# The last image's last stages, row block by row block beside the last scan

## The chip, the cores and the metric

The kernel runs on one core of one Trainium2 chip. The metric is the device time of one launch in microseconds (us); the figure given for a kernel is the median of several runs. The profile is one execution recorded by the hardware profiler, and its times count from the start of its span.

Engines are named as in the profile: PE (TensorE, with PEld for its weight loads), DVE (VectorE), ACT (ScalarE), POOL (GpSimd) and SP (SyncE). SP issues nearly all DMAs of this kernel, in program order.

## The reference

Four images of 96 channels and 64 x 64 points pass through four residual layers. Layer 0 is an attention block, layer 1 and layer 3 each contain a state-space scan in four directions, layer 2 is a 3 x 3 convolution. What matters here is the end of layer 3, after its scan. `oy` holds the four directions; 0 and 2 run along rows (forward and backward), 1 and 3 along columns:

```
y = oy[:, 0] + inv[:, 0] + why + invwhy               # sum over the four directions, 192 channels
y = layernorm_last(y) ; x1 = (y * silu(z)) @ ow.T     # to 96 channels
y = x1 + x2 * g ; y = layernorm over the channels
# crm: squeeze to 24 + 24 channels, a grouped 3x3 convolution, two 1x1 ones,
#      softmax over the channel means of the whole image, a weighted sum
out = y @ fin_w.T + fin_b ; x = x + out
```

Everything up to the convolution works on points; the convolution needs the neighbouring image rows; the softmax needs the means over the whole image, and the output comes after it. The order in which the four directions are added does not matter for what is computed.

## The kernel before, in words

An image is a tile of 96 partitions by 4096 points; 192 channels are two halves `h`. Small stages work on eight chunks of 512 points, that is eight image rows each (`PCH`).

**The scans.** There are eight scans (`SCANS`: layer 1 and layer 3 of each image), each made of 32 groups: four directions, four chunks of 1024 points, two halves. A group has 12 steps, so a scan has 384 steps and the program 3072. A step is `unit(i)`: it asks for the decay tile `rep` of step i+4 (`fetch`, L1807), makes the decays of step i+2 on ACT (`decays`, L1815), runs the scan itself on DVE (`scan`, L1836), multiplies by the output coefficients on POOL (`times_c`, L1848), lets PE sum three steps (`collect`) and spread the inputs of step i+2 into the PSUM tile `bx` (`drive`), and multiplies on DVE (`times_b`, L1829). After a group, `output` forms `yo` and the store to `y_row` or `y_col` in DRAM goes out one step later (L1884). Backward directions first read back what the forward one stored (L1858) and add to it. The order of directions is written out in `KINDS`; for both layers rows come first, columns last.

**The work beside.** The other stages of the images are generators: `first` (layer 0), `second` (end of layer 1, layer 2, start of layer 3) and `third` (end of layer 3). `BESIDE` names which of them run beside which scan. Their code is cut by `yield` into slots. `Slots.begin(budget)` runs one slot ahead of the step's other instructions or in its middle, `end` runs its second half; each slot has a cost, and each step receives `PACE` = 3.5 of budget (less 2.1 in every third step). The generator `prepare`, which makes the inputs of the group after next, is served by the same slots. All instructions of an engine stand in the order in which this program emits them (`manual_schedule`). At step `per - NG - LEAD - 1` = 365 of a scan, `work.run()` emits whatever is left of the work beside it, since the next scan needs its results.

**The end of layer 3.** `third(b)` is `directions` followed by `finish`. `directions` loads the column sums of a half image into `yc` and the row sums into `V`, and POOL adds the turned `yc` to `V` (L1371). `finish` normalizes (`layer_norm`, with `gate` after each chunk), projects, normalizes again (with `squeeze` after each chunk), convolves, sums for the softmax, scales the last weights and writes the output (`o`, L1667, stored in L1669). Each stage goes through all eight chunks before the next begins. The loads of a chunk (`xz`, `x2`, `o`) are issued in the slot that uses them.

The last scan is that of layer 3 of image 3. Beside it run the last stages of images 0, 1 and 2. Those of image 3 need its four directions, so they come after the loop:

```
    solo[0] = True
    spare.clear()
    Slots(third(SCANS[-1][1])).run()
```

Of the kernel before, what the change touches and what calls it, by code (L numbers as in the profile page):

```python
# [9 lines left out]
F32 = mybir.dt.float32  # L10
# [8 lines left out]
L = H * W  # L19
# [18 lines left out]
BESIDE = ((("first", 1),), (("second", 0),), (("second", 1),), (("first", 2),),  # L38
          (("first", 3),), (("second", 2),), (("second", 3),), (("third", 0), ("third", 1), ("third", 2)))
GN_EPS = 1e-5  # L40
# [853 lines left out]
def streams(ctx: ExitStack, tc: tile.TileContext, x, wts, cst, out, wat, cat, flag):  # L894
# [226 lines left out]

    def layer_norm(pool, V, n, gains, each):

        acc = held()
        sq = {}

        def add(j):
            for h in range(n):
                mm(acc[:8], cv("means")[:96, n - 1, 7 - j : 15 - j], sq.pop((j, h)),
                   j == 0 and h == 0, j == 7 and h == n - 1)  # L1130

        for j in range(8):
            js = bass.ts(j, PCH)
            p1 = bank()
            for h in range(n):
                mm(p1[:96], mean[n][:96], V[:, h, js], h == 0, h == n - 1)
            yield
            for h in range(n):
                nc.vector.tensor_sub(V[:, h, js], V[:, h, js], p1[:96])
                t = pool.tile([96, PCH], F32, name="ln_sq", bufs=2 * n)  # L1140
                nc.scalar.activation(t, V[:, h, js], AF.Square)
                sq[j, h] = t
            yield n
            if j:
                add(j - 1)
                yield
                yield n
        add(7)
        yield
        r = pool.tile([8, PCH], F32, name="ln_r", bufs=1)  # L1150
        nc.scalar.activation(r, acc[:8], AF.Sqrt, bias=eps[:8])
        yield n
        nc.vector.reciprocal(r, r)
        yield 3
        for j in range(8):
            js = bass.ts(j, PCH)
            p = bank()
            mm(p[:96], ident[:8, j : j + 1].to_broadcast([8, 96]), r)
            yield
            for h in range(n):  # L1160
                nc.vector.scalar_tensor_tensor(out=V[:, h, js], in0=V[:, h, js], scalar=gains[:, h : h + 1],
                                               in1=p[:96], op0=ALU.mult, op1=ALU.mult)
            yield 1
            yield from each(j)
# [210 lines left out]
    def second(b):  # L1375
# [90 lines left out]
        with tc.tile_pool(name="p2r", bufs=1) as R2:  # L1466
# [57 lines left out]
            with tc.tile_pool(name="p2d", bufs=1) as pool:  # L1524
# [10 lines left out]
                yield from in_conv(pool, "l3_", b, w, x1)  # L1535

    def third(b):

        with tc.tile_pool(name="p3x", bufs=1) as PX:
            V = yield from directions(PX, b)  # L1540
            yield from finish(PX, b, V)

    def finish(PX, b, V):
        with tc.tile_pool(name="p3", bufs=2) as pool:
            w = staged(pool, "l3_in", "l3_out")

            def gate(j):
                js = bass.ts(j, PCH)
                xz = pool.tile([96, PCH], F32, name="xz", bufs=2)
                nc.sync.dma_start(out=xz, in_=gate3[b][:, js])  # L1550
                for h in range(2):
                    p = bank()
                    mm(p[:96], w["l3_in"][:, E + 96 * h : E + 96 * h + 96], xz)
                    yield
                    nc.scalar.activation(p[:96], p[:96], AF.Silu)
                    nc.vector.scalar_tensor_tensor(out=V[:, h, js], in0=V[:, h, js],
                                                   scalar=wv("l3_ss_outn_b")[:, h : h + 1], in1=p[:96],
                                                   op0=ALU.add, op1=ALU.mult)
                    yield 1

            yield from layer_norm(pool, V, 2, wv("l3_ss_outn_g"), gate)
            for j in range(8):
                js = bass.ts(j, PCH)
                x2 = pool.tile([96, PCH], F32, tag="tmp", name="x2")
                nc.sync.dma_start(out=x2, in_=skip3[b][:, js])
                p = bank()
                for h in range(2):
                    mm(p[:96], w["l3_out"][:, h, :], V[:, h, js], h == 0, h == 1)
                yield
                nc.vector.scalar_tensor_tensor(out=V[:, 0, js], in0=x2, scalar=0.5, in1=p[:96],  # L1570
                                               op0=ALU.mult, op1=ALU.add)
                yield 2
        with tc.tile_pool(name="p4", bufs=2) as pool:

            up = pool.tile([96, PADW, W], F32, name="up", bufs=1)
            for s in (up[:, 0, :], up[:, PADW - 1, :], up[0:32, :, 0:1], up[64:96, :, W - 1 : W]):
                nc.gpsimd.memset(s, 0.0)
            sq3 = pool.tile([96, 3, 32], F32, name="sq3", bufs=1)
            nc.gpsimd.memset(sq3, 0.0)
            gw = pool.tile([96, 3, C], F32, name="gw", bufs=1)  # L1580
            nc.gpsimd.memset(gw, 0.0)
            pw = pool.tile([96, C], F32, name="pw", bufs=1)
            n, m, _ = wat["l3_gwc"]
# [6 lines left out]
            nc.gpsimd.tensor_tensor(gw[32:56, 1, :], gw[32:56, 1, :], pw[32:56], ALU.add)  # L1590
            low = pool.tile([24, L], F32, name="low", bufs=1)

            def squeeze(j):
# [12 lines left out]
                q = bank()  # L1606
                mm(q[:24], wv("l3_sq")[:, 1, :], v)
                yield
                nc.scalar.copy(low[:, js], q[:24])
                yield 1  # L1610

            yield from layer_norm(pool, V[:, 0:1, :], 1, wv("l3_ln_g"), squeeze)
            w = staged(pool, "l3_y2", "l3_fin")

            sums = pool.tile([96, 2, 8], F32, name="csums", bufs=1)
            for j in range(8):
                js = bass.ts(j, PCH)
                p = bank()
                for t in range(3):
                    mm(p[:96], gw[:, t, :], up[:, 8 * j + t : 8 * j + t + 8, :], t == 0, t == 2)  # L1620
                    if t < 2:
                        yield (1,)
                yield
                nc.scalar.activation(V[:, 0, js], p[:96], AF.Identity, bias=wv("l3_gwc_b"),
                                     accum_out=sums[:, 0, j : j + 1])
                yield 1
                q = bank()
                mm(q[:96], w["l3_y2"][:24], low[:, js])
                yield
                nc.scalar.activation(V[:, 1, js], q[:96], AF.Identity, accum_out=sums[:, 1, j : j + 1])  # L1630
                yield 1
            mean_ = small.tile([96, 2], F32, name="cmean")
# [26 lines left out]
            for j in range(8):  # L1659
                js = bass.ts(j, PCH)  # L1660
                o = pool.tile([96, PCH], F32, tag="tmp", name="o")
                nc.sync.dma_start(out=o, in_=res2[b][:, js])
                p = bank()
# [8 lines left out]

    NG = 96 // 8
    KINDS = {"l1_": ((0, "r", False), (1, "r", True), (2, "c", False), (3, "c", True)),
             "l3_": ((0, "r", False), (2, "r", True), (1, "c", False), (3, "c", True))}
    groups = [(s, b, tag, k, axis, back, c, h) for s, (tag, b) in enumerate(SCANS)
# [209 lines left out]
    AHEAD, BEHIND, LEAD = 4, 2, 6  # L1886
    PACE = 3.5
    total = len(groups) * NG
    per = total // len(SCANS)
    store, waiting = [], []  # L1890

# [11 lines left out]
    def unit(i, prep, work, budget):  # L1903
# [4 lines left out]
        while store:  # L1908
            store.pop()()
        catch_up(1)  # L1910
        j = i - BEHIND - 2
# [29 lines left out]
    class Slots:  # L1941
# [5 lines left out]
        def begin(self, budget):  # L1947
# [4 lines left out]
            used = 0  # L1952
            v = next(self.stage, 0)
            while isinstance(v, tuple):
                used += v[0]
                if used >= budget:
                    return used
                v = next(self.stage, 0)
# [14 lines left out]
    def beside(s):  # L1973
        stages = {"first": first, "second": second, "third": third}
        for n, b in BESIDE[s]:
            yield from stages[n](b)
# [3 lines left out]
    with tc.manual_schedule():  # L1980
# [15 lines left out]
        for i in range(total):  # L1996
            s, at = divmod(i, per)
            g, m = divmod(i, NG)
            if at == 0:
                work, owed = Slots(beside(s)), 0.0  # L2000
            if m == NG - LEAD and g + 2 < len(groups):
                prep.run()
                prep = Slots(prepare(g + 2))

            if at == per - NG - LEAD - 1:
                work.run()

            owed = min(owed, 0.5) + PACE - (2.1 if i % 3 == 1 else 0.0)
            owed = unit(i, prep, work, owed)
        for j in range(total - 3, total, 3):  # L2010
            collect(j)
            output(j)()
    solo[0] = True
    spare.clear()
    Slots(third(SCANS[-1][1])).run()

# [47 lines left out]
```

## Time and profile before

| | |
|---|---|
| median of 3 runs | 15068.81 us (15060.3 to 15096.54) |
| the profiled execution's own time | 15038.64 us |
| its span | 15036.8 us, mean granted PE clock 0.809 |
| first stages of image 0, alone | 0 to about 830 us |
| the eight scans with work beside | about 830 to 14757 us |
| last stages of image 3, alone | about 14757 us to the end |
| span of the last scan | about 12784 to 14757 us |

The page gives busy times of the whole span first; its second part shows them in 40 slices. A row of the stretches view gives the same for a chosen piece of the span. In the groups of instructions a row is: line, engine, operation, written tile `<-` read tiles, shapes, count, then busy time and mean ns of one, then the idle time of the engine just before them and what ended most of it. Nearly all matmuls have the line of a helper, L948, and are told apart by their tiles. A row of the timeline is start, length, then the instruction, and in brackets the idle time before it.

### The profile page before, as it was taken

What the parts mean: (1) busy time and instruction counts of PE and PEld (TensorE: products, weight loads), DVE (VectorE), ACT (ScalarE), POOL (GpSimd) and SP (SyncE); (2) the same over time, 40 slices, a digit from 0 to 9 for tenths busy, and PEclk for the clock granted to TensorE, in tenths of its full rate; (3) what the DMA queues carried; (4) which work ended last, traced back from release to release, by engine and by line L of the source; (5) the groups of instructions that cost most, each with busy time, mean ns of one, the idle gap of its engine ahead of it and who ended that gap; (6) DMA issues with size and microseconds to landing.
All of it is one profiled execution on the core that took longest, in us unless ns stands there. A gap on an engine that the chain in (4) does not pass through costs nothing. (4 is left out here: it accounts for less than half of the span.)

```text
span 15036.8 us, 127166 instructions
## 1 busy us (share of the span) xinstructions
PE 12260.5 (82%) x40658; PEld 3344.2 (22%) x40658; DVE 11679.2 (78%) x7517; ACT 8280.8 (55%) x11648; POOL 10375.2 (69%) x4746
## 2 busy tenths in 40 slices
PE   8978886888969787889868887897969888667757
PEld 2322221222212222222212221221212222111111
DVE  0067888888878888778887798798878888777784
ACT  3155555555745566555655556455755567545652
POOL 0056787777868777668776787786777778666672
PEclk9978886898969888789867797797879888667666
DMA  0066788786878778667876788687877868666682
GB/s 9 26 149 163 177 202 213 175 211 171 215 178 203 195 183 209 167 168 197 208 179 158 170 204 222 174 203 180 203 195 192 203 173 221 168 166 167 167 204 68
DMA packets 902136, 2644.32 MB, mean 176 GB/s; under 512 B 107280, under 2 KB 257392, under 8 KB 901456
## 3 DMA queue, kind: packets, MB, share of 16 engines
q1 hardware_dynamic: 900800, 2634.83, 71.0%
q8 instruction: 323, 5.29, 0.2%
q14 instruction: 357, 2.92, 0.1%
q10 hardware_dynamic: 656, 1.27, 0.0%
HBM read 2169.08 MB, written 466.62 MB: 175 GB/s over the span
## 5 line engine op out<-in xcount | busy, mean ns | idle before, releaser
L1848 POOL TENSOR_TENSOR rep<-hs,bc 128x1024 f32<-128x1024 f32 x3072 | 7230.5, 2358 | 3160.0 <-DVE hs L1836 2682.5
L1836 DVE TENSOR_TENSOR_SCAN hs<-rep,carry,bx 128x1024 f32<-128x1024 f32 x2304 | 5401.4, 2344 | 277.9 <-POOL rep L1848 15.0
L1829 DVE TENSOR_TENSOR bx<-bx,bc 128x1024 f32<-128x1024 f32 x3072 | 3720.1, 1211 | 1033.6 <-PE bx L948 998.6
L1815 ACT ACTIVATE rep<-rep,l_decay 128x1024 f32<-128x1024 f32 x3072 | 3495.9, 1143 | 903.6 <-DMA rep<-dd 883.7
L948 PE MATMUL bx<-parts,spread 24*128 24x512 bf16 x6144 | 1413.5, 438 | 1812.0 <-DVE hs L1836 1762.5
L948 PE MATMUL acc<-rep,ct 128*32 128x512 f32 x12288 | 2603.0, 732 | 184.9 <-POOL rep L1848 184.9
L1836 DVE TENSOR_TENSOR_SCAN hs<-rep,bx 128x1024 f32<-128x1024 f32 x768 | 1754.2, 2284 | 306.9 <-POOL rep L1848 224.9
L948 PEld LDWEIGHTS <-spread 24*128 24x128 bf16 x6144 | 310.1, 93 | 4297.8 <-DVE hs L1836 2925.5
L948 PE MATMUL one<-band,dg 96*96 96x512 f32 x2304 | 1117.9, 621 | 0.0
L948 PE MATMUL one<-upad,diag 96*96 96x512 f32 x2016 | 1021.0, 643 | 3.2 <-ACT ur L1114 2.7
L948 PEld LDWEIGHTS acc<-rep,ct 128*32 128x32 f32 x12288 | 507.5, 126 | 1958.9 <-issue 1482.0
L948 PE MATMUL one<-qq,kk 96*128 96x512 f32 x1152 | 820.7, 802 | 133.8 <-ACT ex L1234 80.1
L1234 ACT ACTIVATE ex<-one 128x512 f32<-128x512 f32 x576 | 342.8, 595 | 754.1 <-PE one L948 749.3
L948 PE MATMUL one<-pr,ct 6*96 6x512 f32 x1024 | 647.1, 732 | 29.7 <-ACT pr L1720 4.1
L1815 ACT ACT_TABLE_LOAD x470 | 603.0, 1283 | 116.4 <-DMA rep<-dd 108.7
L948 PE MATMUL one<-hp,diag 96*96 96x512 f32 x1152 | 606.5, 665 | 48.0 <-POOL diag L1075 48.0
L948 PE MATMUL one<-vpad,diag 96*96 96x512 f32 x1200 | 590.7, 627 | 0.0
L1844 ACT COPY carry<-hs 128x1 f32<-128x1 f32 x2304 | 408.8, 177 | 314.4 <-DVE hs L1836 313.5
L948 PE MATMUL held<-ex,cols 128*32 128x256 f32 x3072 | 569.2, 451 | 12.0 <-ACT ex L1234 6.0
L948 PE MATMUL held<-ex,vT 128*32 128x256 f32 x3072 | 569.4, 451 | 0.0
L948 PEld LDWEIGHTS one<-band,dg 96*96 96x96 f32 x2304 | 350.6, 166 | 532.7 <-issue 517.1
L948 PEld LDWEIGHTS one<-upad,diag 96*96 96x96 f32 x2016 | 317.6, 172 | 490.0 <-issue 472.6
(3399 smaller groups left out, 13980.7 us busy)
## 6 DMA issues: line engine op xcount, KB each, us to landing
rep<-dd SPq DMA_DIRECT2D x3072, 512.0 KB
parts<-du SPq DMA_DIRECT2D x1024, 144.0 KB
bc<-rows SPq DMA_DIRECT2D x256, 512.0 KB
dd<-delta SPq DMA_DIRECT2D x256, 384.0 KB
du<-cut SPq DMA_DIRECT2D x256, 384.0 KB
us<-urow SPq DMA_DIRECT2D x128, 384.0 KB
du<-cut SPq DMA_DIRECT2D x256, 192.0 KB
yrow<-yo SPq DMA_DIRECT2D x128, 384.0 KB
```

What stands on the lines that cost most here:

```text
L948: nc.tensor.matmul(o, lhsT=lhsT, rhs=rhs, start=first, stop=last)
L1234: nc.scalar.activation(last.rearrange("p a b -> p (a b)"), p, AF.Exp, scale=HD**-0.5)
L1815: nc.scalar.activation(a, a, AF.Exp, scale=decay[tag][:, k, NG * h + m : NG * h + m + 1])
L1829: nc.vector.tensor_mul(bx, bx, ready[i // NG][2][:, 0, :])
L1836: nc.vector.tensor_tensor_scan(out=hs, data0=a, data1=bx, initial=carry[:, h, m : m + 1] if c else 0.0, op0=ALU.mult, op1=ALU.add)
L1844: nc.scalar.copy(carry[:, h, m : m + 1], live[i][1][:, CH - 1 : CH])
L1848: nc.gpsimd.tensor_tensor(a, hs, ready[i // NG][2][:, 1, :], ALU.mult)
```

## The change

It has five parts.

1. `KINDS` of layer 3: the two column directions are scanned first, the two row directions last. The backward row direction, the last of all, goes through the image from its end, so its stores complete the image in blocks of 1024 points (two chunks of 512) from the last rows to the first.
2. `BESIDE` gives the last scan a fourth piece of work, `("last", 3)`, and after the loop only `work.run()` is left. `last(b)` waits until the column directions are stored, then loads them and turns them into `V` by ACT copies (where `directions` loads the rows too and adds on POOL). It calls `finish` with four blocks of two chunks. For each block `finish` waits until both halves of the block's row sums are stored, loads them, adds them to `V` on POOL, and takes the block through both normalizations, gate, projection and squeeze; then it convolves every chunk whose neighbours are there. Softmax and output come once, after the last block. A stage that must wait yields `WAIT`: the step goes on without it. `stored` counts the groups whose stores were issued.
3. `finish` is the same code for images 0 to 2, with one block of eight chunks. Its two tile pools are one, so the memsets and weight loads of the convolution stand at its start; `low` and the weights `l3_y2` share partitions 96 to 119 of `up` and `pw`.
4. `Ahead` issues the load of the next chunk when the present one is taken, for `xz`, `x2`, the row sums and `o`.
5. The budget depends on the work: 3.5 beside `first`, 3.6 beside `second`, 3.2 beside `third`. The work starts at step 2 of a scan instead of step 0, and the drain at step 365 is left out in the last scan.

The diff, cut to its core:

```diff
-          (("first", 3),), (("second", 2),), (("second", 3),), (("third", 0), ("third", 1), ("third", 2)))
+          (("first", 3),), (("second", 2),), (("second", 3),), (("third", 0), ("third", 1), ("third", 2), ("last", 3)))
...
-    def layer_norm(pool, V, n, gains, each):
+    def layer_norm(pool, V, n, gains, each, chunks=range(8)):
...
-                t = pool.tile([96, PCH], F32, name="ln_sq", bufs=2 * n)
+                t = pool.tile([96, PCH], F32, name="ln_sq", bufs=4)
...
+    class Ahead:
+        def __init__(self, load, chunks):
+            self.load, self.left = load, list(chunks)
+            self.next = load(self.left.pop(0))
+
+        def get(self):
+            t, self.next = self.next, self.load(self.left.pop(0)) if self.left else None
+            return t
...
-            yield from finish(PX, b, V)
+            yield from finish(PX, b, V, [(0, range(8))])
+
+    def last(b):
+        with tc.tile_pool(name="p3x", bufs=1) as PX:
+            V = PX.tile([96, 2, L], F32, name="V", bufs=1)
+            per_way = 2 * NCH
+            first_ = len(groups) - 4 * per_way
+            while stored[0] < first_ + 2 * per_way:
+                yield WAIT
+            with tc.tile_pool(name="turn", bufs=1) as T:
+                for h in range(2):
+                    t = T.tile([96, W, H], F32, name="yc")
+                    for j in range(4):
+                        nc.sync.dma_start(out=t.rearrange("p a b -> p (a b)")[:, bass.ts(j, CH)],
+                                          in_=y_col[h][b][:, bass.ts(j, CH)])
+                    yield 1
+                    for j in range(8):
+                        nc.scalar.copy(img(V[:, h, bass.ts(j, PCH)]),
+                                       t[:, :, 8 * j : 8 * j + 8].rearrange("p a b -> p b a"))
+                        yield 1
+            yield from finish(PX, b, V, [(first_ + 3 * per_way + 2 * k + 2, (7 - 2 * k, 6 - 2 * k)) for k in range(NCH)])
...
+            todo, there = set(range(8)), {-1, 8}
+            for need, chunks in blocks:
+                while stored[0] < need:
+                    yield WAIT
+                if need:
+                    for h in range(2):
+                        yr = Ahead(loaded("tmp", y_row[h], 3), chunks)
+                        for j in chunks:
+                            v = V[:, h, bass.ts(j, PCH)]
+                            nc.gpsimd.tensor_tensor(v, v, yr.get(), ALU.add)
+                            yield 1
+                xzs = Ahead(loaded("xz", gate3, 2), chunks)
...
+                yield from layer_norm(pool, V, 2, wv("l3_ss_outn_g"), gate, chunks)
+                x2s = Ahead(loaded("tmp", skip3, 3), chunks)
...
+                yield from layer_norm(pool, V[:, 0:1, :], 1, wv("l3_ln_g"), squeeze, chunks)
+                there |= set(chunks)
+                for j in sorted(k for k in todo if k - 1 in there and k in there and k + 1 in there):
...
+            o_s = Ahead(loaded("tmp", res2, 3), range(8))
...
-                o = pool.tile([96, PCH], F32, tag="tmp", name="o")
-                nc.sync.dma_start(out=o, in_=res2[b][:, js])
+                o = o_s.get()
...
-             "l3_": ((0, "r", False), (2, "r", True), (1, "c", False), (3, "c", True))}
+             "l3_": ((1, "c", False), (3, "c", True), (0, "r", False), (2, "r", True))}
...
-    PACE = 3.5
+    PACE = {"first": 3.5, "second": 3.6, "third": 3.2}
...
         while store:
             store.pop()()
+            stored[0] += 1
...
+            if v == WAIT:
+                return budget
...
             if at == 0:
+                work = idle
+            if at == 2:
                 work, owed = Slots(beside(s)), 0.0
...
-            if at == per - NG - LEAD - 1:
+            if at == per - NG - LEAD - 1 and s < len(SCANS) - 1:
                 work.run()
...
-    Slots(third(SCANS[-1][1])).run()
+    work.run()
```

## The prediction

> **What bounds the kernel now.** I read the page's share line first, then the busy time by stretches, because a mean over the span hides that the stages differ. The chain of waits is of no use here: it holds one piece, the last vector operation.
>
> ```profile
> PE 12260.5 (82%) x40658; PEld 3344.2 (22%) x40658; DVE 11679.2 (78%) x7517; ACT 8280.8 (55%) x11648; POOL 10375.2 (69%) x4746
> ```
>
> ```profile
> 14400.00:14757.00 357.00, 186.27 (x624) 33.70 (x624) 341.75 (x207) 169.46 (x240) 302.72 (x133) 0.60 0.87 211
> 14757.00:15036.80 279.80, 219.77 (x338) 51.81 (x338) 66.58 (x95) 66.63 (x120) 24.00 (x25) 0.68 0.11 31
> ```
>
> Columns: stretch, length, then PE, PEld, DVE, ACT and POOL busy, granted clock, DMA share, GB/s. The first row is the end of the last scan with nothing beside it: DVE works 341.75 of 357 us and the DMA engines are 0.87 busy. The second is what comes after it, all of image 3's last stages alone: DVE 66.58, POOL 24 of 279.8 us. These 280 us are what the change goes for. The groups of instructions between 12784 and 14757 us (the last scan) give the price of a step:
>
> ```profile
> L1836 DVE TENSOR_TENSOR_SCAN hs<-rep,carry,bx 128x1024 f32<-128x1024 f32 x288 | 674.3, 2341 | 23.5 <-POOL rep L1848 2.7 <-DVE bx L1829 0.5
> L1829 DVE TENSOR_TENSOR bx<-bx,bc 128x1024 f32<-128x1024 f32 x383 | 463.5, 1210 | 46.3 <-PE bx L948 42.5 <-PE one L948 3.7
> L948 PE MATMUL one<-xz,l_in 96*96 96x512 f32 x96 | 84.3, 992 | 27.7 <-DMA xz<-gate 27.7
> L1667 DVE SCALAR_TENSOR_TENSOR o<-one,wt,o 96x512 f32<-96x512 f32 x24 | 17.9, 747 | 89.5 <-DMA o<-res 49.7 <-PE one L948 29.6 <-issue 10.2
> ```
>
> A step is one scan and one product, 2.34 + 1.21 = 3.55 us of DVE. From the starts of L1836 in the timeline, every twelfth (a group): groups 24 to 31, nothing beside, take (14757.0 - 14400.9)/8 = 44.5 us each, 3.71 a step. Groups 0 to 23, with the three images beside, take 14400.9 - 12784.1 = 1616.8 us, so one image's last stages cost (1616.8 - 24 x 44.5)/3 = 183 us beside a scan, against 280 alone. For the middle image the groups start at 13329.8, 13417.4, 13480.7, 13557.0, 13617.3, 13674.4, 13725.0, 13779.7, and the next at 13865.7: above 44.5 that is 43 + 19 for the directions, 32 + 16 for normalization and gate, 13 + 6 + 10 for the middle, 41.5 for the last eight outputs.
>
> **Part 1, where the slots end up.** I counted every yield of `first`, `second` and `third` through `Slots.begin` and `unit`, with their costs and the budget. For the kernel before the count ends the three images at step 287 of 384; the trace has their last L1667 at 14398.9, just ahead of group 24 (step 288). The count is therefore trusted. With pace 3.2 and a start at step 2 the three end at step 294, the turning of image 3 by group 25.5, and the row blocks, held back by `stored`, at steps 336, 362 and 383. Only the block of chunks 1 and 0, three convolution chunks and the output are left after the scan.
>
> **Part 2, the tail.** It now lasts from the end of the last scan (14753.35 + 2.35 = 14755.7) to 15036.8: 281 us. The new one, from the old one's own pieces: the last product, sums and `yo` 2.35 + 2.4 + 1.2 = 6; store to data read back 6.7:
>
> ```profile
> 14770.82 0.30 SPq L1884 DMA_DIRECT2D ycol<-yo  x1
> 14777.52 11.84 POOL L1371 TENSOR_TENSOR V<-V,yc 96x512 f32<-96x512 f32 x8 [10.19 <-DMA yc<-ycol]
> ```
>
> Row additions: no row has them contiguous; the strided L1371 takes 1.52, half of the 96x1024 L1764 (2.36) is 1.18; I take 1.2, the nearer form, and 3 us for those not hidden. First normalization of two chunks 9.5, root 2.2, reciprocal 3.3: 15. Gate 2 x 6.2 = 12.5. Projection 4.3. Second normalization 11. Squeeze 2 x 6.95 = 14. Three convolution chunks 3 x 3.9 + 2 = 13.7. Softmax 4.5, output 34.4 as now (eight at 3.63, set by the PE, so loading ahead gains nothing there). Sum 125 us, so -156. If the PE stays slow in the short pieces, 140: -141.
>
> **Part 3, what moves beside the scan.** DVE has no room there, so its work counts in full at least: 6.4 us a chunk (9 operations of 0.68 to 0.74) and two reciprocals of 3.33 a block, 19.5 a block, 58 for three. Whole images paid 79 us outside directions and output for the same kind of 58, a factor 1.36: 79 us. The turn replaces 16 POOL additions of 1.52 by 16 ACT copies, priced like `uc<-ur` (1.10 us, 17.6 in all; ACT was busy 169 of 357 us), and halves the loads; its price is the wait for `yc`, with `decays` queued behind the copy on ACT. The directions' first eight steps lost 39; bounds 5 and 39, I take 23, as the loads are half. Each row addition stands ahead of `times_c` on POOL, and its first load, one for each half, is asked for only just before: six waits of 0 to 12 us, 3 each after the slack of `hs`' three buffers: 18. On SP about 40 more issues at 0.4 us pass between the `rep` loads, 16 us over the 430, hidden behind a queue that is fetched four steps ahead; 8 MB more at the 211 GB/s of the row above is 38 us of DMA time, where 13% of the stretch was free (56 us). Together +120; bounds +80 and +190.
>
> Here a rule weighs against the change. It normalizes in four blocks, so image 3 needs eight square roots instead of two: six more, each with a table switch there and back.
>
> ```profile
> 14814.68 1.28 ACT L1151 ACT_TABLE_LOAD   x1
> 14816.19 0.68 ACT L1151 ACTIVATE ln_r<-held,cols 8x512 f32<-8x512 f32 x1 [0.23 <-PE held L948]
> 14816.90 3.34 DVE L1153 RECIPROCAL ln_r<-ln_r 8x512 f32<-8x512 f32 x1 [2.96 <-ACT ln_r L1151]
> ```
>
> The row shows 1.28 us for a load and 0.23 of idle, which ended with the PE. The Trainium skill, ScalarE: Activation LUTs, section What ACT_TABLE_LOAD costs, counts a drain of about 1380 ns on top, 2.66 us a switch. Twelve switches are 15 us by the row and 32 by the page, on ACT, which has the room by either; if DVE waited for all of it the sum would rise by 17. I keep the row, since no drain stands in it.
>
> **Part 4, loads ahead in the three whole images.** `o` and `xz` were asked for in the slot that uses them; now one slot before. An output step then costs what the PE needs: 4 x 0.916 + a third of the sums' 3.6 + 0.5 for `drive` = 5.4 us, 1.7 over an idle step; eight are 14, the softmax stays at about 10, of 41.5 now: -17 an image. Of the 40 us that PE and its weight loads waited for `xz`, half. Sum -51 - 19 = -70; bounds -110 (all of both) and -10 (SP still stands behind each store of `o`, which it waited for 163.8 us in all). Pace 3.2 only spreads this work over 7 more steps: taken as 0. The merged pools' set-up (memsets and weights on POOL and SP) moves but does not grow: 0, hidden in the first slots; uncovered it would be about 4 us an image.
>
> **Part 5, pace 3.6 in `second`.** At step 368 its four scans stop 17.2 to 18.0 us; the three of `first` 7.4 to 9.2. The reason:
>
> ```profile
> 4177.52 3.64 PE L948 MATMUL one<-us,wt 96*38 96x512 f32 x8 [13.93 <-DMA us<-urow]
> ```
>
> The work was not finished until the drain at step 365, so the stores of `u` stood right ahead of the next scan's first loads. At 3.6 my count ends at step 344: 9.5 us saved, four times -38; denser slots on the PE may cost 4 a scan, +16: -22, bounds -38 and +20. Column before row only changes which `u` and `y` are read: 0, as the loads are of equal size and `u_col` is now stored 20 steps earlier. `first` at start 2 ends at 341 instead of 339: 0.
>
> **Sum.** -156 + 120 - 70 - 22 = -128. The profiled execution took 15038.64 us, 1.8 around its span of 15036.8; it would be 14911. The median of the runs is 15068.81, 30 above it; I subtract the same 128: 14941.
>
> **Rivals.** *DVE floor:* the moved work hides as well as its DVE time allows and loads ahead free all they can: bounds -156 + 80 - 110 - 38 = -224, 14845. For: ACT and POOL have room. Against: over the whole images the cost was 1.36 times DVE's own.
> *It doesn't fit:* the third block ends at step 383 of 384 in the count; if waits of `stored` cost a few steps more, a block falls into the tail, worth about 70 us alone instead of 33 beside: 14978, and slips of two blocks 15015.
> *Traded evenly:* the last scan pays for image 3 the full 183 us of a whole image and loading ahead only brings 20: -156 + 183 - 20 - 10, no change.
> *Slower, the POOL wait:* the 12 row additions made beside the scan each wait on POOL for their load, with `times_c` queued behind, then the sums, the release of `rep` and DVE's next scan. The waits view of this scan has one such wait, POOL V L1371 on V<-yrow: 19.4 us. Twelve of them are 233 in place of my 18: -128 + 215 = +87, 15156. It decides from 12 us an addition (no change) and 16 (slower). For: DVE waited 106 us for POOL's product in this scan. Against: a block loads 0.8 MB, a half of the directions 3.1 at once.
>
> **How the numbers follow.** 0.3% of the time, 45 us, is about what a measurement of this kernel can tell from no change. My case 0.60, DVE floor 0.13, not fitting 0.13: all three faster by more, 0.86. Evenly traded 0.09, POOL wait 0.05. The range goes from near the DVE floor (-219) to where even trade begins (-29): 14850 to 15040. It leaves out about half of the floor's case (0.06), half of even trade (0.05) and the POOL wait (0.05).
>
> **What would show it.** After the last L1836 some 125 us should remain, with one block of two chunks. Group 31 should hold work, groups 24 to 31 some 59 us each. The wait of L1667's successor for `res` should be near nothing, the twelve steps around the outputs nearer 70 than 86 us, and step 368 of `second` near 8 us. I am wrong if the last scan grows beyond 2100 us from its 1973, or if several blocks lie behind the scan.

## The result, and the profile after

The changed kernel takes 15023.95 us (median of 11 runs, 15003.84 to 15056.7) against 15064.4 of the kernel before beside it: a ratio of 0.9973, interval 0.9962 to 0.9984. It is about 40 us faster, less than the 0.3% that I had named as the edge of no change. The forecast was 128 us, with a range that began at 29 us below the time before; the measured 15023.95 lies inside the range, because the range reached almost to no change; the gain is a third of what I forecast.

The profiled execution of the changed kernel is a long one: its span of 15054.8 us is 33 above that kernel's median (15023.95, less 1.8 for what a run's time has over its span). A second one (label `again` below) has 15031.6, 3 below its median. The one of the kernel before, 15036.8, is some 26 us below that kernel's median. Differences of spans between two traces must be read with this scatter in mind. From the starts of the scan instruction (L1836 before, L1893 after) the time splits as follows, in us:

| | before | after | again |
|---|---|---|---|
| ahead of the first scan | 830.4 | 819.2 | 819.4 |
| the seven scans with `first` and `second` beside | 11953.7 | 12055.3 | 12035.3 |
| the last scan | 1971.6 | 2053.4 | 2049.6 |
| behind the last scan | 281.1 | 126.9 | 127.3 |

The tail shrank by 154 us. The last scan took 82 or 78 more. The seven scans that came through with nothing but a new start step, a new pace and a new order of directions took 102 and 82 us more. Some of that is only which executions were profiled: 59 us of the difference between the first two columns (26 + 33), 23 of that between the first and the third. Another 11 us came back at the head, since the first scan starts 11 us earlier. The rest is where the gain went.

Here are the stretches of the changed kernel that answer to the two rows shown of before (stretch, length, PE, PEld, DVE, ACT and POOL busy, clock, DMA share, GB/s): the last groups of the last scan, and what is behind it.

```profile
14434.00:14928.00 494.00, 321.64 (x868) 70.80 (x868) 406.14 (x279) 275.01 (x376) 319.24 (x154) 0.67 0.69 168
14928.00:15054.80 126.80, 87.69 (x132) 21.57 (x130) 29.10 (x41) 23.34 (x40) 4.81 (x3) 0.65 0.12 35
```

The eight groups that used to run bare in 357 us with DVE 96% busy now take 494 with DVE 82% busy, and the stretch with an idle DVE is less than half as long. The groups of instructions of the last scan (12874 to 14928 us):

```profile
L1886 DVE TENSOR_TENSOR bx<-bx,bc 128x1024 f32<-128x1024 f32 x384 | 464.5, 1210 | 33.1 <-PE bx L948 32.7 <-PE one L948 0.3
L948 PE MATMUL one<-xz,l_in 96*96 96x512 f32 x120 | 105.5, 1004 | 0.9 <-DVE V L1652 0.8
L1723 DVE SCALAR_TENSOR_TENSOR tmp<-one,wt,tmp 96x512 f32<-96x512 f32 x24 | 17.8, 740 | 32.4 <-PE one L948 14.0 <-DMA tmp<-res 13.6 <-issue 4.7
L1640 POOL TENSOR_TENSOR V<-V,tmp 96x512 f32<-96x512 f32 x14 | 17.7, 1266 | 4.3 <-DMA tmp<-yrow 4.3
L1572 ACT COPY V<-yc 96x512 f32<-96x512 f32 x16 | 16.9, 1072 | 29.3 <-DMA yc<-ycol 29.2
```

L1723 is the output that was L1667: its idle time fell from 89.5 to 32.4 us, and the gate's matmul, which waited 27.7 us for `xz`, waits no more. The row additions L1640 wait 4.3 us in all; 14 of the 16 lie in this window. The stop at step 368 of `second`'s scans, in the timeline of the changed kernel:

```profile
4179.84 1.93 PE L948 MATMUL one<-us,wt 96*38 96x512 f32 x4 [3.90 <-DMA us<-ucol]
```

It waited 13.93 us before and waits 3.90 now. These waits went as the forecast named them; the sum did not.

### The profile page after: what moved, and what is told of

It is laid out like the page before. It is cut to its first block, busy times and chain, and to the rows that moved or that the text cites. A ratio compares the mean times of both kernels' runs of the same rounds, so it can differ in the third digit from the quotient of the medians.

```text
span 15054.8 us, 127249 instructions
## 1 busy us (share of the span) xinstructions
PE 12292.2 (82%) x40658; PEld 3352.9 (22%) x40658; DVE 11694.8 (78%) x7523; ACT 8343.7 (55%) x11704; POOL 10376.6 (69%) x4746
## 3 DMA queue, kind: packets, MB, share of 16 engines
q10 hardware_dynamic: 656, 1.27, 0.0%
## 4 chain that ended last, share of the span: by engine, by line
PE 50%; DVE 20%; ACT 8%; DMA 6%; POOL 6%; issue 6%; SPq 1%; DVEq 0%; POOLq 0%; ACTq 0%
PE one L948 32%; DVE hs L1893 13%; PE acc L948 9%; PE bx L948 7%; DVE bx L1886 5%; POOL rep L1905 3%; PE held L948 2%; DMA rep<-dd 2%; ACT rep L1872 2%; DMA yc<-ycol 1%; ACT L1872 1%; POOL V L1373 1%; ACT ex L1236 1%; ACT L1814 1%; DMA xz<-gate 1%
## 5 line engine op out<-in xcount | busy, mean ns | idle before, releaser
L1893 DVE TENSOR_TENSOR_SCAN hs<-rep,carry,bx 128x1024 f32<-128x1024 f32 x2304 | 5401.8, 2345 | 310.0 <-ACT carry L1901 36.2
L1893 DVE TENSOR_TENSOR_SCAN hs<-rep,bx 128x1024 f32<-128x1024 f32 x768 | 1754.3, 2284 | 339.1 <-POOL rep L1905 228.8
L948 PE MATMUL one<-pr,ct 6*96 6x512 f32 x1024 | 642.5, 725 | 43.7 <-ACT pr L1777 17.5
```

The source lines that it names most:

```text
L948: nc.tensor.matmul(o, lhsT=lhsT, rhs=rhs, start=first, stop=last)
L1893: nc.vector.tensor_tensor_scan(out=hs, data0=a, data1=bx, initial=carry[:, h, m : m + 1] if c else 0.0, op0=ALU.mult, op1=ALU.add)
```

## The experiments

My theory after the first reading: the moved work and the loads ahead gave about what was forecast, and part 5, which I had put at -22 us, cost instead. The rivals: the seven scans' extra time is scatter of one execution; it comes from the column order; or loads ahead were worth much less than I thought. All ratios are to the kernel before, with runs of both on the same chip; 0.001 is 15 us.

### The change again, and part 5 alone

`again` is the changed kernel unchanged.

> The changed kernel once more, beside the kernel before on the same chip, to see which differences between the two traces come back. In the first pair of traces the tail gave -154 us, the last scan +82, the seven earlier scans together +102, while the medians differ by only -40. Theory (the earlier scans lose by the new start and pace): tail -154 +-3, last scan +80 +-10, the seven scans +20 to +60, ratio 0.997. Rival (the seven scans' +102 is only the scatter of one execution): their difference comes back near -22, as predicted, and the last scan has to be longer instead.

Measured: 0.9977, interval 0.9969 to 0.9984, 21 runs. Tail -154, last scan +78, the seven scans +82. They did not come back near -22, so the rival, scatter, is not the answer; they are also above the 20 to 60 that the theory gave them.

`part5_alone` puts the new start and `second`'s pace into the kernel before:

```diff
-    PACE = 3.5
+    PACE = {"first": 3.5, "second": 3.6, "third": 3.5}
...
             if at == 0:
+                work = idle
+            if at == 2:
                 work, owed = Slots(beside(s)), 0.0
...
-            owed = min(owed, 0.5) + PACE - (2.1 if i % 3 == 1 else 0.0)
+            owed = min(owed, 0.5) + PACE[BESIDE[s][0][0]] - (2.1 if i % 3 == 1 else 0.0)
```

> The kernel before with part 5 alone: work starts at step 2, second gets 3.6; third stays at 3.5 and everything else is as before. My prediction's own figure: -22 us (step 368 saves 8 in each of four scans, 4 given back). Theory that part 5 is what failed: +20 to +50 us, ratio 1.001 to 1.003, with the stop at step 368 gone all the same. Rival (the column order or the merged finish costs it): -22, ratio 0.9985.

Measured: 1.003, interval 1.002 to 1.0041, so 45 us slower than before; the seven scans take 12047.8 us, 94 more than in the trace of before (10 of them come back at the head), with rows still first and the old `finish`. Step 368 stops 7.9 to 9.9 us as forecast. This has neither the column order nor the merged `finish`, so those two are not needed to explain the loss.

### Start and pace, each for itself

`start0` is the changed kernel with the start at step 0; `second35` the changed kernel with `second` at 3.5; `pace36_alone` the kernel before with `second` at 3.6.

```diff
-            if at == 0:
-                work = idle
-            if at == 2:
+            if at == 0:
                 work, owed = Slots(beside(s)), 0.0
```

> The changed kernel with work starting at step 0 of a scan again, pace as changed. Theory A (the shift by two steps costs, since all of the three first scans lost 4 to 28 us with nothing else changed in them): faster than the changed kernel by 30 to 60 us, ratio to before 0.993 to 0.995. Theory B (the pace of second costs): no more than 10 us faster, ratio 0.997.

```diff
-    PACE = {"first": 3.5, "second": 3.6, "third": 3.2}
+    PACE = {"first": 3.5, "second": 3.5, "third": 3.2}
```

> The changed kernel with second at 3.5 again, start at step 2. My count leaves 9 yields at the drain, so step 368 should stop some 17 us or more in four scans. Theory A (the shift costs, the pace does not): 30 to 40 us slower than the changed kernel, ratio 0.999 to 1.0. Theory B (denser slots cost as much as the stop saved): same as the changed kernel within 15 us, the gain at step 368 given back in the conv groups 13 to 20.

```diff
-    PACE = 3.5
+    PACE = {"first": 3.5, "second": 3.6, "third": 3.5}
...
-            owed = min(owed, 0.5) + PACE - (2.1 if i % 3 == 1 else 0.0)
+            owed = min(owed, 0.5) + PACE[BESIDE[s][0][0]] - (2.1 if i % 3 == 1 else 0.0)
```

> The kernel before with second at 3.6 alone, start at step 0. My prediction's term for part 5: -22 us, four stops at step 368 of 9 instead of 17.5 us and something given back, ratio 0.9985. If the start alone spoiled the term: -15 to -40, 0.9975 to 0.999. If denser slots cost more than the stop: above 1.0.

Measured: `start0` 0.9942 (0.9928 to 0.9955), about 53 us faster than the changed kernel. `second35` 0.9983 (0.9976 to 0.9989), the same as the changed kernel within the noise: 9 us slower by the ratios, equal by the medians (15035.82 and 15036.1). Step 368 stops 17.2 to 19.8 us again, and that is nearly all given back elsewhere. `pace36_alone` 1.0009 (1.0001 to 1.0017), 14 us slower instead of 22 faster, with step 368 at 7.4 to 8.8. So the pace is worth nothing or a little less than nothing, and the start at 2 is what costs.

Where the start at 2 costs, two pairs of traces with the same pace and the same short stop at step 368 can tell: `start0` against `again`, and `pace36_alone` against `part5_alone`. The waits of DVE in the seven scans (who waited for whom: us in total, times, longest), first of `start0`, then of `again`:

```profile
DVE bx L1886 <- PE bx L948: 814.5, 421, 8.4
...
DVE hs L1893 <- ACT carry L1901: 25.4, 26, 2.0
...
DVE V L1141 <- PE one L948: 16.3, 9, 3.2
```

```profile
DVE bx L1886 <- PE bx L948: 819.0, 427, 8.0
...
DVE hs L1893 <- ACT carry L1901: 50.6, 35, 4.3
...
DVE V L1141 <- PE one L948: 41.1, 15, 7.1
```

The largest row, the wait of `times_b` for `drive`, hardly moved. What grew is the scan's wait for the `carry` that ACT copies, by 25 us, and the wait of the normalization's subtraction (L1141) for its mean, by 25. Some 20 of these first 25 us arose in group 29 of the scans, where the `decays` ahead of the copy on ACT waited for its `rep` load. In the second pair the wait for `carry` grew by 33 us, and the one for `drive` fell by 10. These rows are about what the start costs, but other rows moved both ways, and why the shift makes them was not traced.

### Which start?

The same edit with other steps, in the first seven scans; the last scan starts at 0, where the changed kernel has 2.

```diff
-            if at == 2:
+            if at == (3 if s < len(SCANS) - 1 else 0):
```

> The changed kernel, work starting at step 3 in the first seven scans and at step 0 in the last. Sums on the PE fall on every third step and the budget is cut there (i % 3 == 1), the preparation of a group on every twelfth. Theory phase of three (what costs at step 2 is where the slots fall against every third step): as good as start at 0, some 50 us faster than the changed kernel, ratio 0.994. Theory later start (each step without work is lost, or the phase of twelve counts): no better than start at 2 but for the last scan's 15 us, ratio 0.997.

> The changed kernel, work starting at step 12 in the first seven scans and at step 0 in the last; the count still ends at 351 of first and 354 of second, ahead of the drain at 365. Theory phase of twelve (the slots fall on the same steps of a group as from 0): as good as start at 0, 0.994. Theory later start (idle steps at the head are lost, as DVE's 3.55 us a step cannot be made up): six times as bad as a shift by two, seven scans 20 to 60 us longer than with start 2, ratio 1.0 or above.

> The changed kernel, work starting at step 5 in the first seven scans, at 0 in the last. So far 0 gives 0.994, 2 gives 0.998, 3 gives 0.992, 12 gives 1.002. Theory phase of three plus a price of the later start: 5 falls like 2, so clearly worse than 3 and 6: 0.998 to 1.001. Theory no rule (where the slots meet the preparation and the sums changes with every start, with no period of three): anything between 0.991 and 1.001, and not ordered as 3 < 6 < 5.

> The changed kernel, work starting at step 6 in the first seven scans, at 0 in the last. Theory phase of three: falls like 0 and 3, 0.991 to 0.995, better than 5. Theory later start alone: between 3 and 12, 0.996 to 0.999, and worse than 5. Theory no rule: anything.

| start | ratio | interval | seven scans in its trace, us |
|---|---|---|---|
| 0 | 0.9942 | 0.9928 to 0.9955 | 11984.2 |
| 2 (as changed) | 0.9977 | 0.9969 to 0.9984 | 12035.3 |
| 3 | 0.9917 | 0.9901 to 0.9934 | 11926.2 |
| 5 | 0.9954 | 0.9939 to 0.997 | 12000.5 |
| 6 | 1.0035 | 1.0024 to 1.0046 | 12124.2 |
| 12 | 1.0018 | 1.001 to 1.0026 | 12115.5 |

The theory of a period of three falls: 3 is the best and 6 the worst. So does a price that only grows with the start: 3 beats 0, and 12 is no worse than 6. Six schedules with the same instructions lie within 190 us. Start 3 alone brings the changed kernel to 14931.52 us.

Between the best and the worst, what differs is DVE's idle time ended by the PE: summed over the seven scans it is 1247 us with start 3 and 1439 with start 6, 192 us more, while all idle time grew by 208. The waits of DVE, first of start 3, then of start 6:

```profile
DVE bx L1886 <- PE bx L948: 752.0, 383, 6.8
...
DVE V L1141 <- PE one L948: 51.8, 23, 4.1
```

```profile
DVE bx L1886 <- PE bx L948: 856.6, 452, 8.0
...
DVE V L1141 <- PE one L948: 109.9, 27, 10.9
```

`times_b` waits 105 us more for `drive`, and the normalization's subtraction 58 us more for its mean; the two are most of the 198 us between these traces.

### The order inside a step

In three steps of each group `prepare` is served first and the work's slot only behind `drive`. There its matmul stands behind one that waits for the scan (in the last scan of the changed kernel `drive`'s matmuls stood idle for 454.5 us, 446.9 of it ended by the scan), and its second half comes at once at the step's end. How many slots fall there should depend on the start; they were not counted. This edit puts the work first in those steps, ahead of the sums and `drive`, and the preparation behind:

```diff
-        first_, rest = (prep, work) if 1 <= prep.slots <= 3 else (work, idle)
+        first_, rest = (work, prep) if 1 <= prep.slots <= 3 else (work, idle)
...
-        if first_ is work and budget > 0.9:
+        if rest is idle and budget > 0.9:
...
-            budget -= rest.begin(budget)
+            budget -= rest.begin(max(budget, 0.0) if rest is prep else budget)
...
-        if first_ is not prep:
+        if rest is not prep:
```

> Start at 3 (0 in the last scan), and in the steps where the preparation of a group used to go first the work's slot goes first, ahead of the sums and drive, the preparation behind drive. Theory (slots that meet preparation steps stand behind drive and hold DVE): all starts gain and come together; this one 0.988 to 0.992. Rival (the spread comes from elsewhere on the PE): no gain, 0.991 to 0.995.

> The same with start at 6, which gave 1.0035 with the preparation first. Theory: the spread to start 3 shrinks from 188 us to less than 60, so below 0.996. Rival: it stays 1.002 to 1.006, or its spread to start 3 stays above 120 us.

> The changed kernel itself (start at 2 in all scans) with the work's slot first in the preparation's steps. It gave 0.9977 with the preparation first. Theory: it comes down to the others, 0.989 to 0.994. Rival: within 0.002 of 0.9977.

> The kernel before (start at 0, pace 3.5, image 3 alone at the end), with the work's slot first in the preparation's steps. If the order holds every schedule: 0.990 to 0.996. If the kernel before happened to fall well against the preparation: 0.996 to 1.0. With the drain at step 365 still there, the stop at step 368 of second stays.

| kernel | preparation first | work first | interval | gain, us |
|---|---|---|---|---|
| start 3 | 0.9917 | 0.9892 | 0.9874 to 0.991 | 38 |
| start 2 (as changed) | 0.9977 | 0.9911 | 0.9895 to 0.9927 | 99 |
| start 6 | 1.0035 | 0.9928 | 0.9913 to 0.9944 | 161 |
| kernel before | 1 | 0.9954 | 0.9938 to 0.997 | 69 |

The edit also gives the work the first call on a step's budget, but the work's last vector operation comes at most three steps earlier by it. The spread between starts 3 and 6 shrank from 188 us to 70 (14962.05 - 14891.95), a little over the 60 that I had set. Among the three starts of the changed kernel, the worse one gained more. The waits of DVE with start 6 and the work first:

```profile
DVE bx L1886 <- PE bx L948: 762.5, 459, 9.9
...
DVE V L1141 <- PE one L948: 113.6, 28, 10.9
```

The wait for `drive` is 94 us shorter, nearly down to start 3's; the wait for the mean has stayed, and is about the size of what is left of the spread. Only start 6 shows this: in the other three pairs of traces the wait for `drive` grew, by 36 us with start 3, 4 with start 2 and 24 in the kernel before. What fell in all four is DVE's idle time ended by the PE as a whole, by 60 to 184 us. Part of the gain is something else, though: the preparation's first matmul, which waits for `us` at the head of a scan, no longer stands ahead of `drive`. Steps 364 to 383 of the seven scans took 591.8 us in the kernel before and 540.0 with the work first; with start 3 it is 544.2 and 511.8, with start 6 546.1 and 510.8. In the kernel before I had expected the stop at the head of the scans behind `second` to stay; it fell from 17.2 to 18.0 us to 7.1 to 9.2. Taking this out, the order itself is worth about 5 us at start 3, 17 in the kernel before, 62 at start 2 and 125 at start 6. These figures subtract differences of single traces from differences of ratios, so 5 and 17 are not told from nothing.

### Loads ahead, and the move, each for itself

`ahead_only` is the kernel before with `Ahead` for `xz`, `x2` and `o`:

```diff
-                xz = pool.tile([96, PCH], F32, name="xz", bufs=2)
-                nc.sync.dma_start(out=xz, in_=gate3[b][:, js])
+                xz = xzs.get()
...
+            o_s = Ahead(loaded("tmp", res2, 3), range(8))
...
-                o = pool.tile([96, PCH], F32, tag="tmp", name="o")
-                nc.sync.dma_start(out=o, in_=res2[b][:, js])
+                o = o_s.get()
```

> The kernel before with loads ahead alone (xz, x2 and o of the end of layer 3), two pools and pace 3.5 as before. My prediction's figure for the three images beside the last scan: -70 us, the twelve steps around the outputs at 70 instead of 86 us, ratio 0.9953. Rival (the prediction's term was too large because the outputs are held by more than the load): -20 to -40, ratio 0.9975, the waits for res and gate gone but the stores of o still waited for on SP.

Measured: 0.9962 (0.9948 to 0.9976), 57 us; the last scan went from 1971.6 to 1915.2, -56. The three output groups take 71.3, 70.2 and 72.7 us, 46 less than before together. In the groups of its last scan:

```profile
L948 PE MATMUL one<-xz,l_in 96*96 96x512 f32 x96 | 81.0, 955 | 0.3
...
L1692 DVE SCALAR_TENSOR_TENSOR tmp<-one,wt,tmp 96x512 f32<-96x512 f32 x24 | 17.8, 741 | 43.4 <-PE one L948 33.8 <-DMA tmp<-res 9.7
```

The loads no longer hold the outputs (9.7 of 49.7 us left); what holds them is mostly the PE (33.8 us), as the forecast's 5.4 us a step had it.

`nolast` is `start0` with image 3's last stages whole and alone behind the loop again:

```diff
-          ..., (("third", 0), ("third", 1), ("third", 2), ("last", 3)))
+          ..., (("third", 0), ("third", 1), ("third", 2)))
...
-    work.run()
+    Slots(third(SCANS[-1][1])).run()
```

> The changed kernel with start at 0, but image 3's last stages whole and alone after the loop again (directions and one block), as in the kernel before; the three other images keep loads ahead, one pool and pace 3.2. Compared with start at 0 (0.9942) this gives the worth of the move by itself: my prediction's -156 + 120 = -36 us, so this one at 0.9966. Rival (the move is worth nothing, as the last scan pays 139 for 154): 0.995 or below.

Measured: 0.9971 (0.996 to 0.9983) against 0.9942 of `start0`: the move by itself is worth 40 us by the medians (15011.82 - 14972.15), forecast 36.

### Pace of third, and everything together

`start3_third35` is start 3 with the pace of `third` put back; `best_of_all` is that with the work first.

```diff
-    PACE = {"first": 3.5, "second": 3.6, "third": 3.2}
+    PACE = {"first": 3.5, "second": 3.6, "third": 3.5}
```

> The changed kernel, start at 3 (0 in the last scan) and third back at 3.5. Loads ahead alone, at pace 3.5, shortened the last scan by 56 us, together with pace 3.2 and one pool only by 45. Theory that pace 3.2 costs: 10 us faster than start at 3 with 3.2 (0.9917), so 0.991. Rival that the one pool costs it: 0.9917 or above. The slots of image 3 end at the same steps in the count (336, 361, 383).

Measured: 0.9904 (0.9889 to 0.9919), 14 us by the medians; the intervals overlap. The last scan took 2028.4 us. Five traces have the same last scan with 3.2 (starts 0, 3, 5, 6 and 12 of the scans before it), and it took 2034.8 to 2049.1 us in them, so 3.5 is 6 to 21 us shorter. Pace 3.2 seems to give back a part of what the loads ahead brought.

> Start at 3 (0 in the last scan), work's slot first in the preparation's steps, third at 3.5. Start at 3 alone 0.9917, with third 3.5 0.9904, with work first 0.9892. If they add up: 0.988. If pace 3.5 and the order take the same waits away: 0.989.

Measured: 14845.1 us, 0.9854 (0.9833 to 0.9876), 220 us faster than the kernel before and about 180 faster than the change. The steps add up, and by the ratios a little more than that (0.988 was expected); in the traces the span is 30 us below that of `work_first_3`, 21 of it in the last scan. Its time behind the last scan is the change's, 124.8 us.

## Why the prediction was wrong, point by point

**Part 1, the slots: right.** In the trace the third image's last output lies in the sixth step of group 24, count 294. One block, three convolution chunks and the output came behind the scan, and the third block's last matmul starts at 14926.05, 2 us ahead of the scan's end.

**Part 2, the tail: right.** 126.9 us for 125. Store to data read back took 5.75 us instead of 6.7, in the timeline of the changed kernel:

```profile
14935.03 0.31 SPq L1941 DMA_DIRECT2D yrow<-yo  x1
...
14940.78 2.48 POOL L1640 TENSOR_TENSOR V<-V,tmp 96x512 f32<-96x512 f32 x2 [10.40 <-DMA tmp<-yrow]
```

**Part 3, the moved work: right.** Groups 26 to 31 take 367.9 us, 101 over bare groups, 34 a block; forecast were 79 + 18 for three, 32 a block. The turn made three long steps, 10.5, 9.4 and 12.0 us in groups 24 and 25, 21 us over idle ones, for 23. The row additions took 1.27 us for 1.2. Their waits were 4 us in all and not 18; so the rival that put 19.4 on each fell by its own row. The sum came out by some luck: as these waits did not come, the moved work itself took about 100 us for three blocks and not 79. The drain of about 1380 ns behind a table load, which the forecast quoted from the Trainium skill, ScalarE: Activation LUTs, section What ACT_TABLE_LOAD costs, does not show here: in the trace of the changed kernel the next ACTIVATE starts 12 ns behind the load in the median of 1015.

**Part 4, loads ahead: the mechanism right, the size too large.** -56 alone for -70: the output groups gave 46 of the 51, so all else, the wait for `xz` included, gave 10 of the 19. In the changed kernel groups 0 to 23 lost 57 us and 16 of the outputs' cost went over into group 24: -41. Pace 3.2, which I took as 0, is probably a part of the difference: with 3.5 the last scan was 6 to 21 us shorter.

**Part 5: this step failed.** I wrote -22, and at its end "`first` at start 2 ends at 341 instead of 339: 0". The stop at step 368 went from 17.5 to 9 us as forecast, four times 8.5. But the pace brought +14 us by itself (`pace36_alone`) and the two together +45 (`part5_alone`); in the changed kernel the start costs 53. I checked only whether the work ends in time and took its place against the steps as free. It is not: the instructions are the same, but how they fall against the steps decides how long DVE waits for the PE and for ACT. With start 2 it is the waits for `carry` and for the normalization's mean that grew; which slot against which step makes them is open. The term goes in the other direction too: with start 3, and 0 in the last scan, the same change takes 14931.52 us. That this is near the 14941 that I forecast is luck, since the pace term and part 4 are as wrong there.

**The sum, with what was measured:** -154 for the tail, +122 for the moved work (101 + 21), -41 for the three images: -73. The medians say -40. So the seven scans and the head of the program cost about +33 where I had -22, and that is 55 of the 88 us that I missed; of the other 33, 29 are part 4.

Of the range of reasons, what is shown is that the start step costs, in the changed kernel and in the kernel before; that between starts 3 and 6 the difference is DVE waiting for the PE; and that the order inside the preparation's steps carries most of the spread between these two. For the start at 2 itself the rows that grew are known, but not why. Which slot meets which step, and why the mean of the normalization waits longer at start 6 under either order, was not traced.

## What to carry to other kernels

When one program interleaves two streams of work by counting slots, a shift by a few steps is an edit of its own: try several before judging anything else by a measurement, because here it moved the time by up to 1.2% while the change under study was worth 0.3%. Look at which of the streams stands first in the queue of the engine that the other one waits for (here changing that order gave 38 to 161 us), and try putting what may wait for a load behind the instruction that feeds the busiest engine. Price a move by the stage that it goes into: here the tail gave 154 us and the filled scan took 122 back.

## What the runs showed of the hardware that was not expected

A POOL addition of 96x512 took 1.27 us with contiguous operands, 1.52 with one turned. The granted clock of the PE went with the schedule although the program's matmuls were the same: 0.802 with start 6, 0.806 as changed, 0.813 with start 3, 0.818 in the best. An ACT table load took 1.28 us, and the next ACTIVATE followed 12 ns later in the median. Whether it is a cause or an effect of DVE's waits was not tried.
